# Attention block of a transformer layer: two query heads in each 32-row group, squares ahead of the rotary turn, no interleaved step in the last round of a group

## The chip, the core and the metric

The kernel runs on one core of a Trainium2 chip. A core has five engines that run side by side: TensorE (PE in the profile, its weight loads PEld), VectorE (DVE), ScalarE (ACT), GpSimd (POOL) and SyncE (SP, which here only issues DMAs). Matmul results land in PSUM, a small memory of eight banks; everything else lies in SBUF. The metric is the device time of one execution in microseconds (us). Before the change the median of three runs is 686.99 us (686.0 to 687.66).

## What is computed

One layer in float32: layernorm, attention with 16 query heads and 4 key/value heads, then layernorm and a mixture of 60 experts with a shared expert. The change touches the attention alone:

```python
B, T, C = x.shape                                  # 2, 1024, 256
q = rms_norm(jnp.dot(x, q_kernel))                 # x here is the layernormed input
k = rms_norm(jnp.dot(x, k_kernel))
v = jnp.dot(x, v_kernel)
q = q.reshape(B, T, K, G, H)                       # K = 4 key heads, G = 4, H = 16
k = k.reshape(B, T, K, H)
...
q = (q * qcos + rotate_half(q) * qsin)             # rotary turn, the same for k
logits = jnp.einsum('btkgh,bskh->bkgts', q * scale, k)
probs = softmax(logits)
encoded = jnp.einsum('bkgts,bskh->btkgh', probs, v)
x = x + jnp.dot(encoded.reshape(B, T, N * H), out_kernel)
```

`rms_norm` runs over the whole row of all heads, so it is one factor for each token.

## The kernel before

Tokens lie in 16 tiles of 128 (8 for each of the two batches), in four **sets** of four tiles. `project` (line 258) makes queries, keys and values of one set: it projects with the transposed input as weights (line 272; `pk` is keys and values of four tiles in one bank, `pq` is the queries of two tiles), turns keys and queries by the rotary table `rope_sb`, finds the norm factors `rqk` by three Newton steps on VectorE (`norm`, line 294, with `rsqrt_of`, line 97), and transposes the result through TensorE into `kT` and `qT`, where head features lie in the partitions. `values` scales the values into `vaug`, and that tile also holds columns of ones, so that the same matmul gives the softmax denominator.

A head has 16 features and the score matmuls (line 496) contract over a group of 32 partitions, one group for each of the four key heads. Before the change the upper 16 rows of each group are zeros: the queries go through the padded tiles `qpad`, the keys through `kpad`, and `qT` has four slices, one for each of the four query heads of a key head. Each token tile thus takes four query transposes (line 474) and a set takes 16, plus four for its keys (line 365).

The attention itself is a list `order` of 128 **rounds**: batch, half of the queries (512), two indices `jp` and `jj` that together pick one of the four query heads of every key head, and `s`, the key tile, innermost, with eight values. Eight rounds with `s` from 0 to 7 are a group. In each round TensorE does four score matmuls for the round after (`ahead`), then `fill(r)` emits at most one step of work that is interleaved, then TensorE does the four matmuls of `av` for this round (line 1030). ScalarE turns scores into exponentials with two activations of 128x1024 (line 511). The scores have three PSUM buffers of two banks (`ps_sc`), `av` has one, and the interleaved work shares one (`ps_misc`). After the last round of a group, `group_end` (line 523) copies `av` out on VectorE before the next group can use the bank.

The interleaved steps are Python generators: the second set (`late`), then sets three and four, then output projections (`out_step`), then the expert routing of finished tiles. The order on TensorE, ScalarE, VectorE and GpSimd is the order in which the program issues, by hand; nothing is reordered in this part. The first set is made ahead of the first round, with `project(..., first=True)`, with matmuls on the identity (`warm`) between its steps. In this **prologue**, ScalarE copies the banks of the query projections to `u` in SBUF (`take`, line 410), squares them for the norm, GpSimd multiplies the swapped halves by the sine (line 424), VectorE does the cosine half and the addition (`turn`, line 431), and each tile's queries are scaled, transposed and copied one after another.

After the last round come the shared expert (line 814), the 60 experts in turn and the end, which the change leaves as they are.

Of the kernel before, what the change touches and what calls it, by code (L numbers as in the profile page):

```python
# [16 lines left out]
P = 128  # L17
# [34 lines left out]
def attention_moe_kernel(  # L52
# [63 lines left out]
    nc.gpsimd.memset(share, 1.0 / C)  # L116
    make_identity(nc, ident)
# [29 lines left out]
    qpad = [pj.tile([P, G, NKV, 32], F32, name=f"qpad{i}", bufs=1) for i in range(2)]  # L147
    kpad = [pj.tile([P, RB, NKV, 32], F32, name=f"kpad{i}", bufs=1) for i in range(2)]

    vaug = att.tile([P, NT, NKV, 3 * H], F32, name="vaug")  # L150
    for t in (kpad[0], qpad[0], qpad[1]):
        nc.gpsimd.memset(t, 0.0)
# [80 lines left out]
    qT = [(qk0, att)[b].tile([P, G, T], F32, name=f"qT{b}") for b in range(B)]  # L233
    kT = [(qk0, att)[b].tile([P, T], F32, name=f"kT{b}") for b in range(B)]
# [12 lines left out]
    def center():  # L247

        mean = any_bank(3 * P, "wmean")
        for c in range(CC):  # L250
            nc.tensor.matmul(
                mean, lhsT=share, rhs=wqkv_sb[:, c, :], start=c == 0, stop=c == CC - 1
            )
        nc.vector.tensor_tensor(
            wqkv_sb, wqkv_sb, mean[:, None, :].to_broadcast([P, CC, 3 * P]), ALU.subtract
        )

    def project(tiles, bank, first):
# [3 lines left out]
        copy = nc.scalar.copy if first else nc.vector.tensor_copy  # L262
        of = slice(tiles[0], tiles[-1] + 1)
        set_ = tiles[0] // RB
        b, c0 = tiles[0] // TPB, tiles[0] % TPB * P
        hh = H // 2
        turns = ((0, hh, H), (hh, 0, H + hh))
        rope_of = rope_sb[:, tiles[0] % TPB : tiles[0] % TPB + RB, :]

        def project_to(to, i, c0, n):  # L270
            for c in range(CC):
                nc.tensor.matmul(
                    to,
                    lhsT=xT_sb[:, c, i * P : (i + 1) * P],
                    rhs=wqkv_sb[:, c, c0 : c0 + n],
                    start=c == 0,
                    stop=c == CC - 1,
                )

        pqs = {}  # L280

        def queries_of(k):

            pqs[k] = bank(2 * NH * H, f"pq{tiles[k]}").rearrange("p (t n) -> p t n", t=2)
            for t in range(2):
                project_to(pqs[k][:, t], tiles[k + t], 0, NH * H)

        def variance(k, n):
            for i in tiles[k : k + n]:
                row_stats(acc[:, i, :], mv[:, i, :], i)  # L290
            if k + n == RB:
                nc.vector.tensor_scalar_add(ss[:, 2, of], mv[:, of, 1], LN_EPS)

        def norm(a, n):

            v = small.tile([P, 3, RB], F32, tag="ms", name=f"ms{set_}_{a}")[:, 0:n]
            for s in range(n):
                if a + s == 2:
                    nc.vector.tensor_copy(v[:, s], ss[:, 2, of])
                else:  # L300
                    nc.vector.scalar_tensor_tensor(
                        v[:, s],
                        ss[:, 2, of],
                        (RMS_EPS, H * RMS_EPS)[a + s],
                        ss[:, a + s, of],
                        ALU.mult,
                        ALU.add,
                    )
            rsqrt_of(rqk[:, a : a + n, of], v)

        if set_ > 1:
            for k in range(0, RB, 2):
                variance(k, 2)
                yield
        elif not first:
            variance(0, RB)
# [4 lines left out]
        if first:  # L321
            variance(0, RB)
            for k in range(0, RB, 2):
                queries_of(k)
        kv = pj.tile([P, RB, 2, NKV, H], F32, tag="kv", bufs=1, name=f"kv{set_}")
        copy(kv.rearrange("p t w g h -> p t (w g h)"), pk)
        uk = kv[:, :, 0]
        k1 = pj.tile([P, RB, NKV, H], F32, tag="k1", bufs=1, name=f"k1_{set_}")
        k2 = pj.tile([P, RB, NKV, H], F32, tag="k2", bufs=1, name=f"k2_{set_}")

        def square_keys():

            sq = pj.tile([P, RB, NKV * H], F32, tag="sqk", bufs=1, name=f"sqk{set_}")
            of_k = uk.rearrange("p t g h -> p t (g h)")
            nc.vector.scalar_tensor_tensor(sq, of_k, 1.0 / NKV, of_k, ALU.mult, ALU.mult)
            nc.vector.tensor_reduce(ss[:, 1, of], sq, AX.X, ALU.add)

        def turn_keys():

            nc.vector.tensor_tensor(  # L340
                k1, uk, rope_of[:, :, None, 0:H].to_broadcast([P, RB, NKV, H]), ALU.mult
            )
            for to, fr, s0 in turns:
                nc.vector.tensor_tensor(
                    k2[:, :, :, to : to + hh],
                    uk[:, :, :, fr : fr + hh],
                    rope_of[:, :, None, s0 : s0 + hh].to_broadcast([P, RB, NKV, hh]),
                    ALU.mult,
                )
            nc.vector.tensor_add(kpad[set_ % 2][:, :, :, 0:H], k1, k2)  # L350

        def values():
            for k, i in enumerate(tiles):
                to = vaug[:, i].rearrange("p g (w h) -> p g w h", w=3)[:, :, 0:3:2, :]
                fr = kv[:, k, 1][:, :, None, :].to_broadcast([P, NKV, 2, H])
                r = rqk[:, 2, i : i + 1]
                if first:
                    nc.scalar.activation(to, fr, AF.Copy, scale=r)
                else:
                    nc.vector.tensor_scalar_mul(to, fr, r)  # L360

        def keys():
            tp = bank(RB * P, f"ktp{set_}").rearrange("p (t n) -> p t n", t=RB)
            for k in range(RB):
                nc.tensor.transpose(
                    tp[:, k, :], kpad[set_ % 2][:, k].rearrange("p g h -> p (g h)"), ident
                )
            copy(kT[b][:, c0 : c0 + RB * P], tp.rearrange("p t n -> p (t n)"))


        if first:
            turn_keys()
            square_keys()
        elif b == 0:
            turn_keys()
            square_keys()
            norm(1, 2)
            values()
            yield
            keys()  # L380
            yield
        else:
            square_keys()
            yield
            norm(1, 2)
            yield
            values()
            nc.vector.tensor_tensor(
                uk.rearrange("p t g h -> p t (g h)"),
                uk.rearrange("p t g h -> p t (g h)"),  # L390
                rqk[:, 1, of, None].to_broadcast([P, RB, NKV * H]),
                ALU.mult,
            )
            yield
            turn_keys()
            yield
            keys()
            yield

        u = pj.tile([P, RB, G, NKV, H], F32, tag="u", bufs=1, name=f"u{set_}")  # L400

        t2 = pj.tile([P, RB, NH, H], F32, tag="t2", bufs=1, name=f"t2_{set_}")

        def heads(k):
            return u[:, k].rearrange("p j g h -> p (j g) h")

        def cos(k, n):
            return rope_of[:, k, None, 0:H].to_broadcast([P, n, H])

        def take(k):  # L410

            copy(u[:, k : k + 2].rearrange("p t j g h -> p t (j g h)"), pqs[k])  # L412
            for i in (k, k + 1):
                sq = pj.tile([P, G, NKV, H], F32, tag="sq", bufs=1, name=f"sq{tiles[i]}")
                ms = ss[:, 0, tiles[i] : tiles[i] + 1]
                f = 1.0 / (NH * H)
                if first:
                    nc.scalar.activation(sq, u[:, i], AF.Square, scale=f**0.5, accum_out=ms)
                else:
                    nc.vector.scalar_tensor_tensor(  # L420
                        sq, u[:, i], f, u[:, i], ALU.mult, ALU.mult, accum_out=ms
                    )
                for to, fr, s0 in turns:
                    nc.gpsimd.tensor_tensor(  # L424
                        t2[:, i, :, to : to + hh],
                        heads(i)[:, :, fr : fr + hh],
                        rope_of[:, i, None, s0 : s0 + hh].to_broadcast([P, NH, hh]),
                        ALU.mult,
                    )

        def turn(k):
            q1 = pj.tile([P, NH, H], F32, tag="q1", name=f"q1_{tiles[k]}")
            nc.vector.tensor_tensor(q1, heads(k), cos(k, NH), ALU.mult)
            nc.vector.tensor_add(t2[:, k], q1, t2[:, k])

        if first:
            for k in range(0, RB, 2):
                take(k)
# [916 lines left out]
```

## Time and profile before

| what | value |
|---|---|
| median of three runs | 686.99 us |
| the profiled execution: its time | 687.18 us |
| the same execution: span on the core | 685.1 us |
| TensorE busy | 669.6 us, 98% |
| VectorE, ScalarE, GpSimd busy | 367.6, 356.7, 190.2 us |
| first score matmul starts | 25.72 us |
| last `av` matmuls end | about 357.2 us |

The span is what lies between the first and the last instruction; about 2 us of the execution's time lie outside it. Busy shares are averages over three very different stages: a prologue of 26 us, attention of 331 us, and the experts. In a timeline each line is start, length, engine, source line, operation, written tile, read tiles, shape and count, and in brackets how long the engine had been idle before and which instruction ended that. A float32 matmul is two records, so `x8` are four matmuls of the program.

### The profile page before, as it was taken

How to read it: one execution, taken by the hardware profiler on the slowest of the kernel's cores; microseconds unless marked ns; L12 is line 12 of the kernel's file. 1: busy time of each engine (PE TensorE's matmuls, PEld its weight loads, DVE VectorE, ACT ScalarE, POOL GpSimd, SP SyncE). 2: the span in 40 equal slices, each digit the busy share in tenths (PEclk: the TensorE clock that was granted, in tenths of full speed). 3: DMA queues.
4: the chain of work that ended last, by engine and by line, in shares of the span. 5: the costliest groups of instructions: out<-in, count | busy, mean ns of one | idle time of the engine just before them, and what ended most of it. 6: DMA issues, size and time to landing. Idle time of an engine off the chain costs nothing. (4 is left out here: it accounts for less than half of the span.)

```text
span 685.1 us, 12519 instructions
## 1 busy us (share of the span) xinstructions
PE 669.6 (98%) x4194; PEld 380.5 (56%) x4195; DVE 367.6 (54%) x1403; ACT 356.7 (52%) x499; POOL 190.2 (28%) x259
## 2 busy tenths in 40 slices
PE   8899999999999999999999998999999999999997
PEld 8433333332224323233225567998898889985466
DVE  4656684823035286446648764444454445443884
ACT  2567787779987687867872510333333333332110
POOL 5020100200000034433045253344544455443000
PEclk9999999999999999999999999999999999999999
DMA  8999930030000011111011076698989888933951
GB/s 283 289 284 298 333 101 1 1 132 1 1 1 1 1 42 50 66 49 59 0 58 58 16 261 229 206 290 293 311 281 295 285 287 299 293 110 105 306 178 52
DMA packets 64275, 106.33 MB, mean 155 GB/s; under 512 B 7417, under 2 KB 51209, under 8 KB 64210
## 3 DMA queue, kind: packets, MB, share of 16 engines
q1 hardware_dynamic: 55010, 86.57, 39.0%
q0 software_dynamic: 7680, 17.32, 7.4%
q10 hardware_dynamic: 1520, 1.64, 0.7%
q8 instruction: 33, 0.54, 0.3%
q14 instruction: 32, 0.26, 0.2%
HBM read 64.13 MB, written 42.45 MB: 156 GB/s over the span
## 5 line engine op out<-in xcount | busy, mean ns | idle before, releaser
L496 PE MATMUL sc<-qT,kT 32*128 32x512 f32 x1024 | 159.8, 639 | 1.9 <-DVE qT L479 0.9
L511 ACT ACTIVATE ex<-sc,rqk 128x1024 f32<-128x1024 f32 x128 | 134.4, 1111 | 37.8 <-PE sc L496 36.2
L1030 PE MATMUL av<-ex,vaug 128*32 128x512 f32 x1024 | 137.3, 604 | 2.0 <-DVE den L537 1.3
L511 ACT ACTIVATE ex<-sc 128x1024 f32<-128x1024 f32 x128 | 124.0, 1021 | 28.9 <-PE sc L496 26.0
L884 POOL DMA_INDIRECT yt<-ys,dst x96 | 93.0, 969 | 115.2 <-ACT ys L1169 75.9
L496 PEld LDWEIGHTS sc<-qT,kT 32*128 32x128 f32 x1024 | 52.4, 183 | 110.1 <-issue 68.6
L1162 PE MATMUL ye<-w,hbuf 128*128 128x256 f32 (+5 forms) x384 | 93.3, 381 | 0.0
L690 POOL DMA_INDIRECT xg<-xs,idx x64 | 63.3, 989 | 93.9 <-DVE idx L685 68.6
L814 PE MATMUL sg<-x2T,ws_sb 128*128 128x512 f32 x176 | 78.1, 596 | 1.1 <-ACTq L1240 1.1
L868 PE MATMUL gua<-xT,w 128*128 128x128 f32 (+5 forms) x480 | 73.2, 295 | 0.5 <-DVE xT L1150 0.5
L868 PEld LDWEIGHTS gua<-xT,w 128*128 128x128 f32 x480 | 70.1, 191 | 4.9 <-issue 0.6
L1169 ACT COPY ys<-ye 128x256 f32<-128x256 f32 (+5 forms) x60 | 29.9, 499 | 75.6 <-PE ye L1162 62.1
L1162 PEld LDWEIGHTS ye<-w,hbuf 128*128 128x128 f32 (+5 forms) x384 | 58.9, 164 | 14.5
L876 DVE TENSOR_TENSOR hbuf<-hbuf,gua 128x128 f32<-128x128 f32 (+5 forms) x60 | 18.9, 315 | 82.5 <-ACT hbuf L875 35.1
L1030 PEld LDWEIGHTS av<-ex,vaug 128*32 128x32 f32 x1024 | 20.4, 107 | 76.5 <-issue 66.7
L814 PEld LDWEIGHTS sg<-x2T,ws_sb 128*128 128x128 f32 x176 | 32.6, 190 | 38.9 <-issue 35.8
L875 ACT ACTIVATE hbuf<-gua 128x128 f32<-128x128 f32 (+5 forms) x60 | 18.0, 299 | 59.8 <-PE gua L868 44.6
L824 ACT ACTIVATE hs<-sg 128x512 f32<-128x512 f32 (+1 forms) x24 | 14.3, 597 | 59.2 <-PE sg L814 57.0
L424 POOL TENSOR_TENSOR t<-u,rope_sb 128x128 f32<-128x128 f32 x32 | 16.9, 558 | 99.1 <-DVE u L412 61.7
L836 PE MATMUL so<-ws_sb,hs 128*128 128x256 f32 x192 | 42.5, 381 | 1.5 <-DVE acc L844 1.5
L868 PE MATMUL gub<-xT,w 128*112 128x128 f32 (+5 forms) x240 | 41.2, 294 | 0.0
L836 PEld LDWEIGHTS so<-ws_sb,hs 128*128 128x128 f32 x192 | 36.2, 190 | 8.2 <-DVE acc L844 2.2
(182 smaller groups left out, 679.0 us busy)
## 6 DMA issues: line engine op xcount, KB each, us to landing
w<-in_wexp_dram SPq DMA_DIRECT2D x60, 624.0 KB
xg<-void SPq DMA_DIRECT2D x60, 221.0 KB
yt<-zero SPq DMA_DIRECT2D x32, 256.0 KB
got<-yt SPq DMA_DIRECT2D x16, 512.0 KB
xe<-xg SPq DMA_DIRECT2D x24, 136.0 KB
xe<-xg SPq DMA_DIRECT2D x10, 170.0 KB
yt<-ys,dst POOLq DMA_INDIRECT x96
xe<-xg SPq DMA_DIRECT2D x8, 187.0 KB
```

Of the source, the lines that this page charges most:

```text
L496: nc.tensor.matmul(sc[:, gg, :], lhsT=kT[b][r : r + 32, s0 : s0 + P], rhs=qT[b][r : r + 32, j, t0 : t0 + QB], start=True, stop=True,)
L511: nc.scalar.activation(ex, sc, AF.Exp, scale=rqk[:, 1, i : i + 1] if b == 0 else 1.0)
L690: s = nc.gpsimd.indirect_dma_start(out=xg[:, :], out_offset=bass.IndirectOffsetOnAxis(ap=at_, axis=0), in_=xs[:, i, :], in_offset=None, bo ...
L814: nc.tensor.matmul(p, lhsT=ws1_sb[:, c, c0 : c0 + P], rhs=x2T[:, c, n * FB : (n + 1) * FB], start=c == 0, stop=c == CC - 1,)
L836: nc.tensor.matmul(po, lhsT=hs[:, m, t * P : (t + 1) * P], rhs=ws2_sb[:, m, :], start=m == 0, stop=m == NC2 - 1,)
L868: nc.tensor.matmul(ps[part][0:m, 0:n], lhsT=w[:, c * W1C + c0 : c * W1C + c0 + m], rhs=xT[:, c, 0:n], start=c == 0, stop=c == CC - 1,)
L875: nc.scalar.activation(h[:, 0, 0:n], ps["ga"][:, 0:n], AF.Silu)
L876: nc.vector.tensor_mul(h[:, 0, 0:n], h[:, 0, 0:n], ps["ua"][:, 0:n])
L884: s = nc.gpsimd.indirect_dma_start(out=yt[:, :], out_offset=bass.IndirectOffsetOnAxis(ap=at, axis=0), in_=y, in_offset=None, bounds_check= ...
L1030: nc.tensor.matmul(av[32 * g : 32 * g + 32, :], lhsT=vaug[:, b * TPB + s, g, H * jj : H * jj + 32], rhs=es[g // 2][:, g % 2, :], start=s == 0,
L1162: nc.tensor.matmul(po[:, t, :], lhsT=h[:, k, t * rows : (t + 1) * rows], rhs=w[:, CC * W1C + k * C : CC * W1C + (k + 1) * C], start=k == 0 ...
L1169: nc.scalar.copy(ys, po)
```

## The change

It does four things.

1. **Packing.** Two query heads that share a key head now lie in the 32 rows of a group: `qT` has two slices and no padding, and the columns of the query weights are put in another order on the host for it. The keys get two copies, `kT[:, 0]` with the key's 16 features in the lower half of a group and zeros above, and `kT[:, 1]` with zeros below and the features above. One padded tile serves both, read at a shift of 16 columns. The score matmul picks the copy by `jj` and the query slice by `jp`; it still contracts over 32 rows. A set now takes 8 query transposes and 8 for its keys; `qpad` is gone.
2. **The first set** has a function of its own, `project_first`. Queries are projected ahead of keys and values. The weights' means are taken off in two pieces (`center(a, b)`). ScalarE squares the queries straight from the PSUM banks, and VectorE turns them straight from the banks, without a copy to `u`; GpSimd keeps one addition. The keys' squares go to ScalarE, the values' scaling to VectorE. All three norms come after both key transposes. The identity matmuls are 5, 11 and 7 in place of 12, 4 and 20.
3. **The other sets.** A step scales one tile's queries, and a later step transposes two tiles at once. The second set's row statistics move behind its keys' turn and squares.
4. **Rounds.** `fill` is not called in rounds with `s` = 7, the last of each group.

A one-column exponential is also issued on ScalarE near the start, behind the first of its three DMAs.

```diff
+    tables = const.tile([P, 1], F32, name="tables")
+    nc.scalar.activation(tables, share[:, 0:1], AF.Exp)
...
-    qpad = [pj.tile([P, G, NKV, 32], F32, name=f"qpad{i}", bufs=1) for i in range(2)]
-    kpad = [pj.tile([P, RB, NKV, 32], F32, name=f"kpad{i}", bufs=1) for i in range(2)]
+    kpad = [pj.tile([P, RB, H + NKV * 2 * H], F32, name=f"kpad{i}", bufs=1) for i in range(2)]
...
-    qT = [(qk0, att)[b].tile([P, G, T], F32, name=f"qT{b}") for b in range(B)]
-    kT = [(qk0, att)[b].tile([P, T], F32, name=f"kT{b}") for b in range(B)]
+    qT = [(qk0, att)[b].tile([P, G // 2, T], F32, name=f"qT{b}") for b in range(B)]
+    kT = [(qk0, att)[b].tile([P, 2, T], F32, name=f"kT{b}") for b in range(B)]
...
+    def keys(tiles, jj, bank, copy):
+        tp = bank(RB * P, f"ktp{tiles[0]}_{jj}").rearrange("p (t n) -> p t n", t=RB)
+        for k in range(RB):
+            nc.tensor.transpose(
+                tp[:, k, :], kpad[tiles[0] // RB % 2][:, k, H - H * jj :][:, 0:P], ident
+            )
+        c0 = tiles[0] % TPB * P
+        copy(
+            kT[tiles[0] // TPB][:, jj, c0 : c0 + RB * P], tp.rearrange("p t n -> p (t n)")
+        )
+    def queries(i, n, q, bank, copy):
+        tp = bank(n * (G // 2) * P, f"qtp{i}").rearrange("p (j t n) -> p j t n", j=G // 2, t=n)
+        for t in range(n):
+            for jp in range(G // 2):
+                nc.tensor.transpose(tp[:, jp, t, :], q[:, t, jp * P : (jp + 1) * P], ident)
+        c0 = i % TPB * P
+        copy(
+            qT[i // TPB][:, :, c0 : c0 + n * P], tp.rearrange("p j t n -> p j (t n)")
+        )
...
+    def project_first():
+        tiles = range(RB)
+        pos = rope_of(tiles)
+        two = [P, 2, NH, H]
+        pq = {}
+        for k in range(0, RB, 2):
+            pq[k] = any_bank(2 * NH * H, f"pq{k}").rearrange("p (t n) -> p t n", t=2)
+            for t in range(2):
+                project_to(pq[k][:, t], k + t, 0, NH * H)
+        variance(tiles)
+        t2 = pj.tile([P, RB, NH * H], F32, tag="t2", bufs=1, name="t2_0")
+        for k in range(0, RB, 2):
+            for t in range(2):
+                sq = pj.tile([P, NH * H], F32, tag="sq", bufs=1, name=f"sq{k + t}")
+                nc.scalar.activation(
+                    sq,
+                    pq[k][:, t],
+                    AF.Square,
+                    scale=(NH * H) ** -0.5,
+                    accum_out=ss[:, 0, k + t : k + t + 1],
+                )
+            of_k = pos[:, k : k + 2]
+            q1 = pj.tile([P, 2, NH * H], F32, tag="q1", name=f"q1_{k}")
+            nc.vector.tensor_tensor(
+                heads(q1), heads(pq[k]), of_k[:, :, None, 0:H].to_broadcast(two), ALU.mult
+            )
+            for to, fr, s0 in TURNS:
+                nc.vector.tensor_tensor(
+                    heads(t2[:, k : k + 2])[:, :, :, to : to + HH],
+                    heads(pq[k])[:, :, :, fr : fr + HH],
+                    of_k[:, :, None, s0 : s0 + HH].to_broadcast([P, 2, NH, HH]),
+                    ALU.mult,
+                )
+            (nc.vector if k else nc.gpsimd).tensor_tensor(
+                t2[:, k : k + 2], q1, t2[:, k : k + 2], ALU.add
+            )
+        pk = any_bank(RB * 2 * NKV * H, "pk0").rearrange("p (t n) -> p t n", t=RB)
+        for k in tiles:
+            project_to(pk[:, k], k, NH * H, 2 * NKV * H)
+        kv, k1, k2 = key_tiles(0)
+        nc.scalar.copy(kv.rearrange("p t w g h -> p t (w g h)"), pk)
+        for k in tiles:
+            sq = pj.tile([P, NKV * H], F32, tag="sqk1", bufs=1, name=f"sqk{k}")
+            nc.scalar.activation(
...
+            )
+        warm(11)
+        turn_keys(tiles, kv[:, :, 0], k1, k2)
+        keys(tiles, 0, any_bank, nc.scalar.copy)
+        keys(tiles, 1, any_bank, nc.scalar.copy)
+        warm(7)
+        norm(tiles, 0, 3)
+        for k in tiles:
+            r = rqk[:, 0, k : k + 1]
+            if k < 2:
+                nc.vector.tensor_scalar_mul(t2[:, k], t2[:, k], r)
+            else:
+                nc.scalar.activation(t2[:, k], t2[:, k], AF.Copy, scale=r)
+        for k in tiles:
+            queries(k, 1, t2[:, k : k + 1], any_bank, (nc.vector.tensor_copy, nc.scalar.copy)[k % 2])
+        values(tiles, kv)
...
+        for jj in range(2):
+            keys(tiles, jj, bank, copy)
+            if b == 0 and jj == 0:
+                norm(tiles, 1, 2)
+                values(tiles, kv)
             yield
...
+                if t % 2 == 0:
+                    yield
             yield
+            queries(tiles[k], 2, t2[:, k : k + 2], bank, copy)
+            yield
...
-                    lhsT=kT[b][r : r + 32, s0 : s0 + P],
-                    rhs=qT[b][r : r + 32, j, t0 : t0 + QB],
+                    lhsT=kT[b][r : r + 32, jj, s0 : s0 + P],
+                    rhs=qT[b][r : r + 32, jp, t0 : t0 + QB],
...
-        warm(12)
-        center()
-        warm(4)
-        early = project(range(RB), any_bank, True)
-        late = project(range(RB, TPB), bank, False)
-        next(early)
-        next(early)
-        warm(20)
-        for _ in early:
-            pass
+        warm(5)
+        center(0, NH * H)
+        center(NH * H, 3 * P)
+        project_first()
+        late = project(range(RB, TPB))
...
-            if r != 1:
+            if r != 1 and s < TPB - 1:
                 fill(r)
...
-    q = a["q_kernel"].reshape(C, NKV, G, H).transpose(0, 2, 1, 3).reshape(C, NH * H)
+    q = a["q_kernel"].reshape(C, NKV, G // 2, 2 * H).transpose(0, 2, 1, 3).reshape(C, NH * H)
```

## The prediction

> **What bounds the kernel now.** I read the page's slices first: TensorE is at 9 tenths or more everywhere but in the first two, so the place to look is the prologue, and then what a round of attention costs. The timeline from 0 gives the prologue (TensorE, ScalarE, VectorE and GpSimd together; most lines left out):
>
> ```profile
> 1.97 5.49 PE L958 MATMUL warm<-ident 128*128 128x128 f32 x24 [1.97 <-POOL ident masks.py:199]
> ...
> 7.25 1.59 PE L251 MATMUL wmean<-wqkv_sb,share 128*128 128x384 f32 x4
> ...
> 9.89 2.05 PE L272 MATMUL pk<-wqkv_sb,xT_sb 128*128 128x128 f32 x16 [0.16 <-DVE wqkv_sb L254]
> ...
> 11.78 3.62 PE L272 MATMUL pq<-wqkv_sb,xT_sb 128*128 128x256 f32 x16
> ...
> 24.04 0.57 ACT L479 COPY qT<-qtp 128x512 f32<-128x512 f32 x1
> ...
> 24.88 0.69 DVE L479 COPY qT<-qtp 128x512 f32<-128x512 f32 x1 [1.35 <-PE qtp L474]
> ...
> 25.72 1.99 PE L496 MATMUL sc<-qT,kT 32*128 32x512 f32 x12 [0.88 <-DVE qT L479]
> ```
>
> No score matmul can start before the last query copy, and 20.4 to 25.6 is a relay: scale, transpose, copy, tile after tile. Everything later waits for 25.72, so time saved here is saved at the end, unless a later stage waits for something else.
>
> Second view, TensorE's timeline inside attention, without and with an interleaved step, and at a group's end:
>
> ```profile
> 153.33 1.06 PE L1030 MATMUL av<-ex,vaug 128*32 128x512 f32 x8
> 154.32 1.14 PE L496 MATMUL sc<-qT,kT 32*128 32x512 f32 x8
> 155.39 1.07 PE L1030 MATMUL av<-ex,vaug 128*32 128x512 f32 x8
> 156.39 1.46 PE L496 MATMUL sc<-qT,kT 32*128 32x512 f32 x8
> 157.78 1.06 PE L1030 MATMUL av<-ex,vaug 128*32 128x512 f32 x8
> ...
> 164.88 1.07 PE L1030 MATMUL av<-ex,vaug 128*32 128x512 f32 x8 [0.50 <-DVE den L537]
> ```
>
> From start to start a bare round is 2.07, then 2.39 with 0.32 inside the score pair, where TensorE waits for ScalarE to free a score bank; two bare rounds take 4.45. A round with four transposes (53.02 to 55.67) is 2.65, and in a run of such rounds nothing waits: the step itself costs 0.58. The first bare round behind a step is 2.07 again. So a step taken away saves 0.58 less the waits that come back.
>
> **Part 1, the prologue.** Each time below is worked from a row.
>
> *Start.* 24 records of warm in 5.49 are 0.229 each, against 0.116 for the 40 at 15.68 (4.63): TensorE is at half rate until about 7.6 (the first wmean record takes 627 ns, the median 486). Ten records end at 4.26. Are the weights there? ScalarE's DMA queue moves its first 192 KB (its half of them) by about 3.8, SyncE's by 3.4. So wmean starts at 4.3; at half rate 4 records of 256 columns are 1.76, and 0.15 of tail: 6.25. The first subtraction (512 of the 768 elements that took 0.95) takes 0.69, and pq starts at 7.0, where pk started at 9.89 before.
>
> *A rule that bears on it.* "TensorE: Matmul & The Clock Gate", Part 1, puts the change of rate about 4 us into sustained activity, and says that about 3.4 us without work bring the half rate back. The rows say 5.6 (1.97 to 7.6). By the rule pq would run at full rate from its start and end at 10.65; by the row two of its records run at 0.44 and 14 at 0.226: 11.1. I take the row. The rule's other half speaks against cutting 12 and 4 to 5: every gap in the first 8 us now counts. Where it does not bite is the end: from 20.84 to 25.7 TensorE had 16 short transposes, and the first scores ran at full rate.
>
> *ScalarE's DMAs.* The one-column exponential puts the table load (1.28 at 2.19 before) ahead of ScalarE's half of `xT_sb` and the rotary table, whose issues go from 1.22 and 1.71 to about 2.8 and 3.3. That half moved from 3.8 to 6.0 before, because the queue was still busy with the weights; I expect its end at 6.4 to 6.8, just ahead of pq. SyncE's queue is not passed by anything. The load was idle time on ScalarE anyway (first work at 11.98), so taking it early gains nothing.
>
> *Banks.* In the built program's order VectorE's first turn waits for ScalarE's squares of the same bank. "PSUM — Partial Sum Buffer", section "PSUM bank collisions raise a hardware error", says why: no two engines may touch one bank and quadrant at once, reads against reads included. So "straight from the banks" is one engine after the other. First bank: 9.4 (two slow records, six fast). Two squares take 1.06 (14.33 to 15.39): 10.55. VectorE would be free at 10.05 (weights' second piece, then statistics that took 2.4 from 9.76), so the rule costs 0.5 here. One multiplication of 512 (0.69, as the 128x512 addition at L558) and two of 256 (0.42 each): 12.2. Second bank: matmuls 11.2, squares 12.3, turn 14.0, addition 0.69, about 14.7. GpSimd adds the first pair meanwhile; 128x128 takes it 0.54, so some 2.2 from 12.2 to 14.4, and VectorE's rows beside a busy GpSimd are longer (L433 0.67 against 0.42), so 0.3 more: 15.0.
>
> *Keys, norm, queries.* pk ends at 13.1, its copy at 13.7; VectorE turns keys in 1.36 (12.60 to 13.96): 16.4. Two key transposes and their copies (0.58 a set on TensorE, 0.57 a copy on ScalarE) end at 18.5, beside the norm. The norm took 3.1 (17.24 to 20.33) beside GpSimd; the one at 34.11 took 2.26 for two factors, so 2.5 for three: 18.9. VectorE and ScalarE then scale two tiles each, 0.62 and 1.0: 19.9. Eight transposes (0.146 each), then copies of 256 in place of 512, about 0.4 each, two on each engine; the last is ScalarE's, behind its scaling: 20.3 transposed, 21.3 copied. **First scores at 21.4 in place of 25.72: 4.3 saved.** Ends: 5.2 (the rate opens early, no lengthening) and 3.0 (weights or inputs 1 us later).
>
> **Part 2, the rounds.** ScalarE's and the score matmuls' work is the same: still 32 rows, still 128x1024. Transposing steps with the first 64 rounds go from 15 (12 for queries, 3 for keys) to 12 (6 and 6). Three steps are 1.74; but the 12 query steps stood in runs of four, without waits, while the six new ones stand two bare rounds apart, so that the 0.32 comes back. Counted round by round with 2.07, 2.39 and the steps in their new places, 0.7 is left over all 128 rounds.
>
> Waits of VectorE: at 37.92 the fifth round waited 0.73 for the second set's key copy behind norm and values; the copy now comes ahead of both, and the statistics behind the keys' turn; by the same rows round 7 starts 22.2 after the first scores, as before, with one more step done: 0.6 gained. One more such wait (0.48 at 129.96) goes, since tiles are scaled a round or two ahead of their transposes. Against it: after each second group VectorE holds `av` for two reads, and the next `av` waits 0.5 (the line at 164.88) unless a step of TensorE lies in the first round of the next group. In rounds 16 and 32 of before such steps lay there; after the change none does: 1.1 lost. Leaving `s` = 7 free moves steps, and removes none; before the change VectorE's share in those rounds was hidden already, so I give it 0. **Sum 0.7 saved**, between -1 and 2.
>
> **Part 3, the rest.** Routing steps come one or two rounds later, so about two more scatters go into the shared expert's steps, where GpSimd has room for them before the last two routes send theirs (GpSimd's gaps between scatters at 373 to 378 are up to 2.3): 0. The clearing of `xg` and `yt` is over by about 110, so the early start meets no transfer that gates it. Everything behind attention shifts.
>
> **Sum.** 4.3 + 0.7 = 5.0 off 687.18, the profiled execution: 682.2. Its time is 0.2 above the median, within the runs' spread, so I forecast **682.2**.
>
> **Rivals.**
> - *The rate opens one window late* (at about 11.0 in place of 7.6; for it: the gap between warm and wmean if the weights land after 4.3; against: bytes moved). Then pq takes nine records of 0.44 and seven of 0.226: end 12.6, 1.5 later, and the chain behind follows, with a little more for the first bank: 684.2. Chance 0.14.
> - *The rounds give it back:* the isolated steps and the emptier last rounds leave a 0.5 wait at every one of 16 group ends, not at the six counted. 10 x 0.5 = 5.0 more: 687.2, no change. For it: the wait exists; against: with `jj` = 0 only one copy of 0.69 stands before the next `av`, beside scores of 1.07. Chance 0.08.
> - *Slower: a cold TensorE.* The input half behind the table load lands near 8, TensorE stands for a stretch, and the half rate holds through the whole prologue. pq then ends at 15.0, pk at 18.7; the 11 identity matmuls, fillers at full rate, take 5.0 and stand in front of the key transposes: 23.7, 26.1 with those, 29.3 with the last 7, scores at 31: 5.3 later than before, 691.8. It decides only if the rate is still half at about 15. For it: fewer fillers early. Against: TensorE is busy without a break from 7 on. Chance 0.06.
> - *It does not do what it says:* the host's column order and the slices agree with each other in the diff, and nothing in the shapes hides work. No chance of its own.
>
> **How the numbers follow.** Forecast 0.72, its own range 680.5 to 683.8 from the ends above; late rate 0.14; no change 0.08; slower 0.06. From 679.8 to 685.2 the range holds the first two and the doubtful ends. A measurement of this kernel can tell about 0.2% (1.4 us) from no change. Faster: 0.72 + 0.14 = 0.86; same 0.08; slower 0.06.
>
> **What would show it.** First scores between 21 and 22 in the new timeline; pq ahead of pk and starting near 7; the first wmean near 4.3, at 0.44 a record; VectorE's first bank multiplication right behind the second square. In the rounds: transposing steps 6 and 6, and waits of 0.5 at the `av` of rounds 16 and 32. The span from first scores to last `av` (331.5 now) should be about 330.8. I am wrong if it grew by more than 1, or if the first scores come after 23.

## The result and the profile after

The changed kernel takes 678.68 us (median of four, 678.47 to 679.25) against 687.33 for the kernel before in the same session (686.0 to 688.7): a ratio of 0.9883, 95% interval 0.9859 to 0.9907. The direction was forecast; the size was 8.4 in the profiled pair (687.18 to 678.74) where 5.0 was forecast, and the time lies below the range of 679.8 to 685.2. The granted clock was 1.0 in both profiled executions.

Two marks in TensorE's timeline cut both spans into three: the first score matmul and the start of the last `av`.

| stage | before | after | saved | forecast |
|---|---|---|---|---|
| start to first scores | 25.72 | 19.82 | 5.90 | 4.3 |
| first scores to last `av` | 329.59 | 327.72 | 1.87 | 0.7 |
| last `av` to the end | 329.79 | 329.36 | 0.43 | 0 |
| outside the span | 2.08 | 1.84 | 0.24 | 0 |

The last two rows lie within the scatter: the profiles below differ by up to 3 us behind attention, for kernels whose code there is the same.

The timeline of all engines in the new prologue, cut to the chain (a transpose is one record, other matmuls are two):

```profile
2.02 2.50 PE L253 MATMUL warm<-ident 128*128 128x128 f32 x10 [2.02 <-POOL ident masks.py:199]
6.91 3.72 PE L274 MATMUL pq<-wqkv_sb,xT_sb 128*128 128x256 f32 x16 [0.34 <-DVE wqkv_sb L262]
9.45 0.38 ACT L383 ACTIVATE sq<-pq 128x256 f32<-128x256 f32 x1
10.34 0.17 DVE L286 TENSOR_SCALAR ss<-mv 128x4 f32<-128x4 f32 x1
10.41 0.69 DVE L392 TENSOR_TENSOR q<-pq,rope_sb 128x512 f32<-128x512 f32 x1
11.02 0.75 DVE L396 TENSOR_TENSOR t<-pq,rope_sb 128x256 f32<-128x256 f32 x2
11.75 0.69 DVE L392 TENSOR_TENSOR q<-pq,rope_sb 128x512 f32<-128x512 f32 x1
11.85 1.28 POOL L402 TENSOR_TENSOR t<-q,t 128x512 f32<-128x512 f32 x1 [1.83 <-DVE t L396]
12.35 0.75 DVE L396 TENSOR_TENSOR t<-pq,rope_sb 128x256 f32<-128x256 f32 x2
13.74 0.42 DVE L320 TENSOR_TENSOR k<-kv,rope_sb 128x256 f32<-128x256 f32 x1
15.24 1.06 PE L345 MATMUL ktp<-ident,kpad 128*128 128x128 f32 x8 [0.37 <-DVE kpad L331]
```

The chain is VectorE's, as forecast. But its first bank starts behind the statistics (L286) and not behind ScalarE's squares, which ended at 9.93. A bank's three products take 1.34 from start to start (10.41 to 11.75), and VectorE's two products beside GpSimd's addition (12.35) are as long as those without it (11.02): 0.75 for both. TensorE runs all of `pq` at full rate: 3.72 for 16 records.

The stalls forecast at rounds 16 and 32 are in TensorE's timeline:

```profile
67.22 1.07 PE L1068 MATMUL av<-ex,vaug 128*32 128x512 f32 x8 [0.50 <-DVE den L586]
110.38 1.06 PE L1068 MATMUL av<-ex,vaug 128*32 128x512 f32 x8 [0.50 <-DVE den L586]
```

### The profile page after: what moved, and what is told of

Read it like the earlier page. It is cut to its first block, busy times and chain, and to the rows that moved or that the text cites. A ratio compares the mean times of both kernels' runs of the same rounds, so it can differ in the third digit from the quotient of the medians.

```text
span 676.9 us, 12425 instructions
## 1 busy us (share of the span) xinstructions
PE 663.9 (98%) x4156; PEld 375.9 (56%) x4157; DVE 361.7 (53%) x1404; ACT 355.7 (53%) x503; POOL 185.7 (27%) x250
## 5 line engine op out<-in xcount | busy, mean ns | idle before, releaser
L506 POOL TENSOR_TENSOR t<-u,rope_sb 128x128 f32<-128x128 f32 x24 | 12.4, 545 | 129.5 <-DVE u L492 129.5
```

## The experiments

Twelve kernels ran, in three sets. The kernel before has medians of 686.25, 684.45 and 687.72 in them, so totals are compared within a set or by ratio. The length of attention, from the first scores to the start of the last `av`, repeats better: the changed kernel gave 327.72 and, run again, 327.73, while two variants of set 2 that leave attention alone gave 328.02 and 328.01. Differences below 0.3 are thus not read there.

### The rounds: packing, steps and the free last round

**Steps at `s` = 7 put back** (set 1), in the changed kernel:

```diff
-            if r != 1 and s < TPB - 1:
+            if r != 1:
```

> The changed kernel with steps allowed in the last round of a group again. The prediction gave the free last rounds 0: then the time stays within 0.3 of 678.7 and attention (first scores to last av) stays at 329.6. Rival: the free last rounds are where the rounds' unpredicted 1.2 come from (VectorE's share of a step stood in front of the reads of av); then attention is 0.5 to 1.2 longer and the time about 679.5.

680.12 (679.7 to 680.95), ratio 0.9894 (0.985 to 0.9938); attention 328.82, which is 1.10 longer: the rival was right. (The 329.6 of the expectation runs to the end of the last `av`, 2.0 behind the mark used here.) Two waits of `av` are new or longer in TensorE's timeline:

```profile
69.66 1.07 PE L1068 MATMUL av<-ex,vaug 128*32 128x512 f32 x8 [0.98 <-DVE ms L296]
93.04 1.06 PE L1068 MATMUL av<-ex,vaug 128*32 128x512 f32 x8 [1.11 <-DVE num L578]
```

They stand in place of the changed kernel's two waits of 0.50 at 67.22 and 110.38, the second of which is gone: 0.98 + 1.11 − 1.00 = 1.09, the whole of the 1.10. VectorE's timeline of the same kernel ahead of the second one:

```profile
91.83 0.16 DVE L108 TENSOR_TENSOR rs_t<-rs_y 128x4 f32<-128x4 f32 x1
92.03 0.16 DVE L109 SCALAR_TENSOR_TENSOR rs_t<-rs_t,ms 128x4 f32<-128x4 f32 x1
92.22 0.16 DVE L110 SCALAR_TENSOR_TENSOR rqk<-rs_t,rs_y 128x4 f32<-128x4 f32 x1
92.30 0.68 DVE L578 COPY num<-av 128x512 f32<-128x512 f32 x1
```

The step of that last round is a norm, a chain of small dependent instructions on VectorE from 89.78 to 92.4, and the copy of `av` stands behind it; the next `av` needs the bank. The step has no work for TensorE at all: its price is paid by the first matmul of the next group. Ahead of 69.66 it is the copy of a projection and the keys' squares, from 66.66 to 68.2, that stand before the two reads of `av`.

**Packing alone** (set 1), in the kernel before: `qT` with two slices, `kT` with two copies, the column order, two key transposes with a step of their own in the rounds; nothing else.

```diff
-            tp = bank(G * P, f"qtp{i}").rearrange("p (j n) -> p j n", j=G)
-            for j in range(G):
+            tp = bank(G // 2 * P, f"qtp{i}").rearrange("p (j n) -> p j n", j=G // 2)
+            for j in range(G // 2):
...
-                    rhs=qT[b][r : r + 32, j, t0 : t0 + QB],
+                    rhs=qT[b][r : r + 32, jp, t0 : t0 + QB],
```

> The kernel before with the packing alone: two heads to 32 rows, two key copies, 2 query transposes a tile, half-size query copies; prologue order, warm counts, interleaving rule as before. By the prediction's sums: 1.74 fewer transposes in the rounds less the waits that come back, about 0.7 to 0.9; in the prologue's relay of four tiles each loses 0.29 of transposes and 0.2 of copy, less one more key transpose and copy beside it, about 1.2. Time about 685.0. Rival: the packing carries most of the 8.4, then below 682.

686.54 (682.49 to 687.59, 20 executions), ratio 0.9985 (0.9969 to 1.0001); four of them at a granted clock of 1.0 gave 682.49 to 683.0, sixteen at 0.992 to 0.998 gave 685.49 to 687.59. The total hides the gain, since most executions lost TensorE's rate (below). The profiled one is of the first kind: attention 328.10, 1.49 less than before, where 0.7 to 0.9 was expected, and 14.86 from `pk` to the first scores where it was 15.83: 0.97 less, with 1.2 expected. With the run above attention divides: packing −1.49; all else that the change does to the steps (scaling one tile, transposing two, the second set's statistics later) +0.72, by difference only, from 328.10 to 328.82; the free last rounds −1.10.

**One copy of `av`** (set 2), in the changed kernel:

```diff
-        nc.vector.copy_predicated(n, odd_sb.to_broadcast([P, QB]), av)
-        nc.vector.stream_shuffle(den2, av, SWAP)
+        held = ends_of.tile([P, QB], F32, tag="held", bufs=1, name="held")
+        nc.vector.tensor_copy(held, av)
+        nc.vector.copy_predicated(n, odd_sb.to_broadcast([P, QB]), held)
+        nc.vector.stream_shuffle(den2, held, SWAP)
```

> The changed kernel with one copy of av to SBUF at the end of every second group, and the two reads then from the copy, so that the bank is free after 0.69 in place of two reads. Five to six stalls of 0.3 to 0.5 stand in TensorE's rounds (behind the groups that end in rounds 15, 31, 47, 63, 79, 95). If they are VectorE's hold on the bank they go, attention is 2.0 to 2.6 shorter and the time 676.3 to 676.8. If the next scores' wait for ScalarE takes their place, under 1.

675.08 (674.7 to 675.43), ratio 0.9871 (0.9854 to 0.9888). Attention 325.95, 1.77 shorter than the changed kernel's and 2.06 shorter than that of the two variants of this set; 2.0 to 2.6 was expected. The changed kernel has five waits of `av` at group ends, of 0.28 to 0.50 and 2.28 in sum; here none is left, although VectorE does one instruction more there. In the timeline of this kernel the next `av` comes behind the copy:

```profile
65.97 0.69 DVE L586 COPY held<-av 128x512 f32<-128x512 f32 x1 [3.51 <-PE av L1070]
66.70 0.75 DVE L587 COPY_PREDICATED num<-odd_sb,held 128x512 f32<-128x512 int32 x1
66.91 1.06 PE L1070 MATMUL av<-ex,vaug 128*32 128x512 f32 x8
```

**That copy and both additions on GpSimd**, then **the same with steps at `s` = 7** (set 3, beside the changed kernel once more). The second edit in `project_first` is:

```diff
-            (nc.vector if k else nc.gpsimd).tensor_tensor(
+            nc.gpsimd.tensor_tensor(
```

> The changed kernel once more, as the reference of this set on its chip. Its prologue and attention should repeat within 0.5: first scores at 19.8 to 20.3 (the time at which TensorE's rate opens moves by some tenths), from there to the last attention matmul 327.7 to 328.0. What follows attention has come to 264.3 to 267.5 up to the last expert's chain, with the chip and not with the kernel, so the median may lie anywhere from 676 to 679; the other three are compared with this one.

> Two further edits on the changed kernel: av is copied once and read from the copy, and GpSimd takes both additions of the first turns. My theory: the stalls of 0.5 at group ends are the two reads of av, and they go (attention 326.0 in place of 327.7, as with the copy alone), and the prologue's chain is VectorE, so its 0.69 addition comes off the first scores (0.6 earlier, near 19.2 to 19.6): 2.4 faster than the changed kernel of this set. Rival: GpSimd's additions, 1.28 each and one after the other, delay the scaling of the third and fourth tile, or VectorE's key turns grow beside them: first scores as before and 1.8 faster only.

> The kernel of the run before this one, with interleaved steps in the last rounds of groups again. Theory A: what a step at s = 7 costs is VectorE's queue: the copy of av stands behind that step's VectorE work, whatever is read afterwards, so two av matmuls wait 0.5 to 1.1 again and attention is 0.6 to 1.1 longer than in the run before. Theory B: the cost is how long av is held, so with the one short copy nothing waits and attention is the same within 0.2.

The changed kernel: 679.5 (678.36 to 682.46), ratio 0.9884 (0.9859 to 0.9908), first scores at 20.08. With both edits: 677.52 (675.88 to 678.07), ratio 0.9845 (0.9821 to 0.9868), attention 325.96: the copy's gain, and nothing from GpSimd, since the first scores came at 20.37. The rival was right, and the timeline of VectorE and GpSimd in that kernel says how:

```profile
12.08 2.68 POOL L402 TENSOR_TENSOR t<-q,t 128x512 f32<-128x512 f32 x2 [1.67 <-DVE t L396]
13.18 0.46 DVE L320 TENSOR_TENSOR k<-kv,rope_sb 128x256 f32<-128x256 f32 x1
13.56 1.55 DVE L324 TENSOR_TENSOR k<-kv,rope_sb 128x128 f32<-128x128 f32 x2
15.22 0.43 DVE L331 TENSOR_TENSOR kpad<-k,k 128x256 f32<-128x256 f32 x1
```

L324's two products take 0.49 in the changed kernel; here they take 1.55. Only the first of them is long (1.35 in place of 0.29): it starts while GpSimd adds, and ends at 14.92, just behind GpSimd, which is done at 14.76. L320 also reads two tiles in SBUF, but was under way before GpSimd's second addition: it took 0.46 (0.42 in the changed kernel), and that addition 1.43 in place of 1.28. So the keys are turned no earlier than without the edit. Of the 2.4 expected 2.0 came, within 0.2 of the copy's 1.8.

With steps at `s` = 7: 679.05 (678.7 to 681.48), attention 327.58, 1.62 longer. Three lines of TensorE's timeline show what the copy changes:

```profile
69.56 1.06 PE L1070 MATMUL av<-ex,vaug 128*32 128x512 f32 x8 [0.23 <-DVE held L586]
76.85 0.66 PE L345 MATMUL ktp<-ident,kpad 128*128 128x128 f32 x4 [0.68 <-DVE kpad L331]
93.70 1.06 PE L1070 MATMUL av<-ex,vaug 128*32 128x512 f32 x8 [1.10 <-DVE num L578]
```

At the first of these group ends, where the short copy stands in place of the two reads, the wait is 0.23 and not 0.98: there Theory B is right. At the last one, where one copy to `num` stood before too, 1.10 are left: there Theory A is right, and VectorE's queue alone makes the wait. And 0.68 comes up where neither had it, at key transposes that wait for VectorE. So the price of 1.62 lies above A's 0.6 to 1.1, although only one `av` waits long.

### The prologue: fillers, banks and order

**12 fillers at the start in place of 5** (set 1), in the changed kernel:

```diff
-        warm(5)
+        warm(12)
```

> The changed kernel with 12 identity matmuls at the start in place of 5, so that the weights' means start when these end. If the rate opens near 5.5 they end near 5.9 and the first scores come about 1 us later (time 679.7); if it opens near 7.6 they end at 7.5 and the first scores come about 2 us later (time 680.7): the fillers cost what they cover, and the first scores' delay is close to the delay of the means.

680.48 (679.75 to 680.87); first scores at 20.97, 1.15 later, `pq` at 8.07 in place of 6.91. So of the 5.9, about 1.15 came from the fillers (the identity matmuls of `warm`) that no longer stand ahead of the weights' means.

About as much is no gain of the change. This kernel and the packed one start with the same 24 filler records as the kernel before. They take 4.40 and 4.47 for them, where the profile of before took 5.49:

```profile
2.02 4.47 PE L963 MATMUL warm<-ident 128*128 128x128 f32 x24 [2.02 <-POOL ident masks.py:199]
```

In these two the records get short near 5.2, in the profile of before at about 7.5. The packed kernel's `pk` thus starts at 8.83 and that of before at 9.89: 1.06 of the 5.9 belong to that one execution. How other executions of the kernel before open is not on record.

**ScalarE copies the banks to SBUF first**, and **turns ahead of the squares** (set 2):

```diff
+            u = pj.tile([P, 2, NH * H], F32, tag="u0", name=f"u0_{k}")
+            nc.scalar.copy(u, pq[k])
+            pq[k] = u
             for t in range(2):
```

> The changed kernel, but ScalarE first copies each query bank to SBUF (two copies of 0.59), and squares and turns read the copy. It asks what 'straight from the banks' is worth. VectorE's first turn started at 10.41, right behind its row statistics, with the bank free since 9.93; the copy is there at about 9.5. ScalarE's chain ends its last square at about 12.4, where its key copy starts anyway. Expected: first scores within 0.3 of 19.82 and time 678.7 to 679.1. Rival: the direct reads carry 1 us or more of the gain, then 679.7 or above.

> The changed kernel with VectorE's turns of each bank issued ahead of ScalarE's squares, so that the squares wait for the turns. The bank is one engine's at a time: squares of the first bank then start at about 11.8 in place of 8.94, those of the second end near 14.2, the key copy starts there in place of 12.45, and the keys' turn, which follows it on VectorE, at 14.85 in place of 13.74. Expected first scores 1.1 to 1.4 later, time about 679.9. Rival: the order is of no weight (within 0.3) since VectorE is the bound.

678.17 (677.63 to 679.53; ratio 0.9912, 0.9894 to 0.993) and 678.07 (677.88 to 678.22; ratio 0.9914, 0.9896 to 0.9931), with first scores at 21.67 and 21.05; the kernel with one copy of `av`, whose prologue is that of the changed kernel, had them at 20.07 in this set. Both are slower prologues, by 1.6 and 1.0. For the copies no difference had been expected, so the rival was right there; the turns came near their 1.1 to 1.4. With the copies VectorE's first product came at 11.19 (10.74 there), behind statistics whose input landed 0.45 later, which is not shown to be the edit's doing. Most of the rest is in these rows:

```profile
11.80 0.75 DVE L399 TENSOR_TENSOR t<-u,rope_sb 128x256 f32<-128x256 f32 x2
12.64 1.64 POOL L405 TENSOR_TENSOR t<-q,t 128x512 f32<-128x512 f32 x1 [1.73 <-DVE t L399]
13.07 1.83 DVE L399 TENSOR_TENSOR t<-u,rope_sb 128x256 f32<-128x256 f32 x2
```

The two products of the first bank take 0.75 from `u`, with GpSimd idle; those of the second take 1.83 beside GpSimd, and in the changed kernel, from the bank, 0.75 beside GpSimd too. So it is the two together that cost: operands in SBUF, and GpSimd at work. Again one product is long (1.49) and ends behind GpSimd's addition, which is itself longer than its 1.28. The Trainium skill, "SBUF — State Buffer", section "Who interferes with whom", has a rule that fits these rows and the one of L324: a VectorE instruction with two SBUF inputs contends with a GpSimd instruction that reads SBUF; one with at most one such input does not, outside VectorE's two-port modes. A product of bank and table has one; a product of `u` or `kv` and table has two.

With the turns first, VectorE gains nothing, as its statistics go on to 10.6 anyway, and ScalarE, whose squares wait until 11.97, copies `pk` at 14.13 (12.56 in the kernel with one copy of `av`): the keys' turn starts at 14.74 in place of 14.00, and the norm behind it then waits for the keys' squares.

### TensorE's rate

**5 fillers in the kernel before** (set 1), and **that with three fillers behind each later tile's query transposes** (set 2):

```diff
-        warm(12)
+        warm(5)
```
```diff
+            if first and k:
+                warm(3)
             if first and k + 1 < RB:
                 queries(k + 1)
```

> The kernel before with 5 identity matmuls in place of the first 12, nothing else. It isolates how much of the prologue's gain is only the early start, and shows when TensorE's rate opens. If the weights are there by 4.3 and the rate opens at about 7.6, as the prediction took from the row of before: weights' means at 0.66 a record, end near 7.0, first projection near 8.0 in place of 9.89, first scores near 23.8, time about 685.1. If the rate opens some 3.5 us after the first matmul (5.5): means end near 6.4, first projection 7.4, first scores 23.3, time about 684.6. If the weights were late, no change.

> The kernel before with 5 identity matmuls at the start, as in the first experiment, and three more behind each of the last three tiles' query transposes, where TensorE otherwise does 0.66 of work in each 1.6. 15 of 20 executions of the first experiment had a granted clock of 0.992 to 0.995 and took 687 to 688.7, five had 0.999 and took 684.3. If the gaps of this relay close TensorE's rate, then with the fillers nearly all executions have 0.999 or 1.0 and take about 684.3 to 684.8. Rival: the dip comes from somewhere else (the first scores' own load); then the two groups stay.

The first gave nothing in the median: 687.67 (684.22 to 688.73, 20 executions), ratio 1.0003 (0.9987 to 1.002). They fall in two groups: five at a granted clock of 0.999 took 684.22 to 684.37, fifteen at 0.992 to 0.995 took 686.98 to 688.73. A table of windows of the profiled one (0.992; columns: window, its length, busy time and count for TensorE, its weight loads, VectorE, ScalarE and GpSimd, then TensorE's granted clock, DMA share, GB/s):

```profile
20.00:22.00 2.00, 0.66 (x4) 0.42 (x4) 1.29 (x3) 0.90 (x3) 0.00 (x0) 1.00 0.91 285
22.00:24.00 2.00, 1.08 (x8) 0.87 (x12) 1.22 (x4) 1.64 (x5) 0.00 (x0) 0.80 0.91 284
24.00:26.00 2.00, 2.00 (x10) 0.83 (x8) 1.63 (x7) 0.30 (x1) 0.00 (x0) 0.50 0.92 285
...
32.00:34.00 2.00, 2.00 (x16) 0.58 (x14) 1.21 (x3) 0.00 (x0) 0.00 (x0) 0.64 0.91 285
```

TensorE's timeline of the same execution, from the last query transposes to the first scores:

```profile
22.05 0.66 PE L474 MATMUL qtp<-ident,qpad 128*128 128x128 f32 x4 [0.95 <-ACT qpad L462]
23.58 5.36 PE L496 MATMUL sc<-qT,kT 32*128 32x512 f32 x16 [0.87 <-DVE qT L479]
```

The first scores start 2.14 earlier than before (1.06 of it is the late opening of the profile of before), but their sixteen records take 5.36 (3.47 in the changed kernel run again, with a wait for ScalarE in it); the rate is half from about 23 to 33, and attention takes 333.26 in place of 329.59. The relay before it left gaps of 0.60, 0.65, 0.95 and 0.87. Fillers in three of these gaps end it: 682.63 (681.73 to 684.52), ratio 0.9967 (0.9954 to 0.9979), all 20 executions at 0.999 or 1.0. The kernel before loses the rate in 21 of its 75 executions in the three sets (clock below 0.9975); in set 1 those have a median of 689.0, the others 686.1. Part of the change's gain in the medians is that it does not lose it: in set 3 the kernel before has 687.72 over all executions and 687.06 over those that kept the rate, against 679.5.

**The changed kernel without its 11 and 7 fillers** (set 3):

```diff
-        warm(11)
...
-        warm(7)
```

> The changed kernel without the 11 and the 7 filler matmuls of its prologue (nothing of the computation is left out). Theory: they keep the rate open, as the fillers in the old relay did. Without them TensorE does 1.06 of transposes between about 12.4 and 17.9, the rate closes in most executions, the first scores take 5.4 in place of 2.0 and the half rate holds for about 10 us: 3 to 4 slower, granted clock 0.992 to 0.995. Rival: one gap of 2.9 and one of 1.6 are too short for the rate to close, nothing is in the fillers' way either: the same within 0.3, clock 0.999.

683.69 (680.0 to 685.5), ratio 0.9924 (0.9899 to 0.995), against 679.5 for the changed kernel beside it: 4.2 slower, and all eight executions at 0.989 to 0.995. The profiled one in TensorE's timeline:

```profile
11.09 1.95 PE L274 MATMUL pk<-wqkv_sb,xT_sb 128*128 128x128 f32 x16
15.87 1.06 PE L345 MATMUL ktp<-ident,kpad 128*128 128x128 f32 x8 [2.83 <-DVE kpad L331]
18.51 1.97 PE L358 MATMUL qtp<-ident,t 128*128 128x128 f32 x8 [1.58 <-DVE t L427]
20.95 5.37 PE L543 MATMUL sc<-qT,kT 32*128 32x512 f32 x16 [0.46 <-DVE vaug L335]
```

The window in which its rate closes, with the columns of the table above:

```profile
18.00:20.00 2.00, 1.49 (x7) 1.33 (x8) 1.04 (x3) 1.24 (x3) 0.00 (x0) 0.59 0.93 328
```

The theory holds, at a little more than the 3 to 4 expected and with the clock below its 0.992 in some executions. The rival had counted on gaps of 2.83 and 1.58 being too short. Without the fillers about half of the change's gain is lost. They cost no time on the path: in the changed kernel TensorE is idle for 0.37 behind the first of them (the line at 15.24), and the query transposes start 0.41 behind VectorE's scaling with them and without. The 41 executions of the changed kernel and its variants with fillers were all at 0.999 or 1.0.

## Why the prediction fell short

**What held.** The chain of the prologue ran as drawn: queries first, VectorE as its bound, keys' turn, norm, a short relay. The three fewer steps (60 transposes in the rounds before, 48 after) and the stalls at rounds 16 and 32 appeared, and the waits of 0.73 and 0.48 that were to go are gone. The rounds without their free ends were put at 0.7, and came to 1.49 − 0.72 = 0.77; the sum agrees, but its parts were not measured one by one. No rival happened: TensorE was neither late nor cold, and the rounds did not give the gain back.

**Where the miss lies.** Of the 3.4 that separate 8.4 from 5.0, 1.6 are in the prologue, 1.2 in the rounds and 0.7 behind attention and outside the span, where the runs scatter. Without that 0.7 the profiled execution would still lie below the range.

**The step that failed: "Leaving `s` = 7 free moves steps, and removes none; before the change VectorE's share in those rounds was hidden already, so I give it 0."** It was worth 1.10 here, and 1.62 in the kernel with one copy of `av`. Hidden it was: in the kernel before no `av` waits ahead of the line at 164.88 (shown in the prediction). But that says nothing of the new order. There a norm and the copy of a projection fall on last rounds, and `av` would wait behind them if those rounds were not free. A step's VectorE work has to be placed in the new order, against what stands behind it on its engine; only its TensorE work was.

**The term mis-sized: VectorE's chain in the prologue.** From its first bank product to the keys' turn the sum had 4.45 (10.55 to 15.0); it took 3.33 (10.41 to 13.74). A bank's three rows add up to 1.53 (0.69 and twice 0.42); the sum has 1.65 and 1.7 for them (10.55 to 12.2, 12.3 to 14.0), more than the rows that it names, and the timeline 1.34 and 1.38, since one VectorE instruction starts up to 0.1 before the one ahead of it ends. 0.3 was added for GpSimd's company, which a product read from a bank did not feel; the wait for the second bank's squares did not come. What was left, 0.14 in the start and 0.3 in keys, norm and relay, makes the 1.6 by which the first scores were early. GpSimd's addition (2.2 forecast, 1.28 measured) was not on the path.

**The rate's opening** was taken at 7.6 from the one row, against the rule of about 4 us in the Trainium skill, "TensorE: Matmul & The Clock Gate", Part 1. In the new profile the fillers and the first half of `wmean` were at half rate until about 5.9, 3.9 behind the first matmul, so the rule was nearer than the row here. It moves from execution to execution: in the fourteen profiles the records get short between about 5.1 and 8.1. In two of the variants' profiles `pq` took 4.24 or 4.25, two records slow, as forecast. In the kernel without its 11 and 7 fillers the second bank's products then wait 0.44 for ScalarE's squares, so this is worth up to some 0.4 and is not the main error. The rule of bank exclusivity was put at 0.5 in the start; the statistics ended later than the squares, so it cost nothing in the changed kernel. With 12 fillers, where `pq` is late, VectorE waits 0.43 for the squares of the first bank. In these profiles the two engines never read one bank at once, so none shows what would come of it.

What stays open: what the second half of the prologue's gain consists of. Of the 5.9, 1.06 is the late opening in the profile of before, 1.15 the fillers at the start and 0.97 packing; the remaining 2.7 is order, banks and the shorter relay together, by difference. Whether the kernel with one copy of `av` gains the 0.72 as well if its steps are grouped as before was not tried. The fastest kernel by the stage marks is the changed one with one copy of `av`: the two variants with it and with free last rounds are 1.8 shorter in attention.

## What to carry over

When interleaved steps are moved, list for each the work that it puts on every engine, and ask what time-critical instruction is queued behind it, above all the one that frees a PSUM bank. Add VectorE chains from start to start, and look at where operands lie before adding a charge for a busy GpSimd. And where a stage has many short matmuls with gaps of under 1 us, look at the granted clock of several executions: a saving ahead of it can be handed back by the rate.

## What the hardware showed unexpectedly

- TensorE dropped to half rate behind a stretch with no gap above 0.95 us, where it was busy for 0.66 of 2.0 us in one window and 1.08 in the next; 15 of the 20 executions have the lower clock. The Trainium skill, "TensorE: Matmul & The Clock Gate", Part 1, gives some 3.4 us without work as the rule, and tells of one kernel whose short idle times between groups of matmuls were enough, without their lengths; here a thin stretch was enough. Once down, the half rate lasted about 10 us (23 to 33) although TensorE was busy throughout from 24.
- The slow matmuls in the first 5.9 us of the changed kernel do not show in the granted clock: its windows read 1.00 there.
- Two products of 128x256 on VectorE took 0.75 beside a busy GpSimd when one operand lay in PSUM, and 1.83 when both lay in SBUF. It is one of the two that is long, until GpSimd's addition has ended.
- The stage behind attention differed by up to 3 us from profile to profile (327.0 to 330.1 from the start of the last `av` to the span's end): 329.1 to 329.4 in set 1, 327.0 to 328.5 in set 2, 328.1 to 330.1 in set 3. Why is not shown.
